# Attention with the batches in turn, and the last 256 tokens as dense slots, in an attention and mixture-of-experts block

## The chip, the cores and the metric

The kernel runs on one core of a Trainium2 chip. The metric is the device time of one execution in microseconds (us). Five engines work side by side, each with an instruction queue of its own: PE (matrix products), DVE (vector operations), ACT (activation functions), POOL (small operations and indirect DMAs) and SP (it issues most DMAs).

## The reference

The input x has 2 batches of 1024 tokens with 128 features. All values are float32. Cut to what matters:

```python
x = x + layernorm(attention(layernorm(x)))      # causal, 8 heads in 2 groups, latent keys and values of 32
x = x + layernorm(ffn(layernorm(x)))

def ffn(h):                                      # per token
    scores = sigmoid(h @ gate_weight.T)          # 32 experts in 4 groups of 8
    # the 2 best groups by the sum of their two best (scores + bias),
    # then the 6 best experts inside these 2 groups
    tw = scores[top6] / sum * 0.2
    routed = sum over the 6 of tw * (silu(h @ w_gate[e]) * (h @ w_up[e])) @ w_down[e]
    shared = silu(h @ shared_w_gate) * (h @ shared_w_up) @ shared_w_down
    anchor = the anchor expert that belongs to the best expert (one of 16)
    return routed + shared + 0.1 * anchor
```

So each token needs two of the four groups of experts, and which two depends on the data.

## The kernel before, in words

A token tile is 128 tokens; there are 8 in each batch, 16 in all. The kernel has four stages.

**Attention.** The work is cut into units (batch b, head group g, 256 queries q), and a unit into q+1 steps of 256 keys. `units` and `steps` fix the order: batch 0 with q = 0 to 3, then batch 1; 40 steps in all. A step has its scores (`numerators`, lines 541 and 555), the exponentials on ACT (561), in the last step of a unit a causal select on POOL (564), and in the following step the products with the values (578) and the sums (587). The maxima that a unit needs are computed ahead by PE (476, 486) and DVE (493). `project(b, c)` makes queries, keys and values of 512 tokens.

**Routing.** `route(i)` is run for each entry of `parts`: output projection (`po`, 712), two norms, transposes (`pt_h`, 746), gate products (`pl`, 752), and the choice of groups and experts on DVE. There are four parts of 4 tiles. Part 0 is not sorted (`ND = 1`), the others are: each token is copied twice into the DRAM tensor `placed`, once for each of its groups, so that each slot of 256 rows (`SL`) belongs to one group. The sorted tiles come in two sets, 8 tiles (`NT0`) and 4 tiles. `place_first` and `place_second` compute the places of a set on POOL (lines 895 to 947), and `move_rows` scatters its rows with indirect DMAs (955), one for each tile and choice.

**Dense pass.** `experts(0, 0)` takes the 512 tokens of part 0 through all four groups (lines 1317, 1318, 1331), with weights `wbd` and spread coefficients `spreadd`.

**Slots.** `Slots` runs 15 slots (`NS`), of which the first 5 (`NS0`) need the first set only. For each slot it fetches rows (`got`, 1095), transposes them (1105, 1107), writes the coefficients to DRAM (`cw_slot`, 1112), reads them back spread over partitions (`spreads`, 1126 and 1131), fetches the group's weights (`wbs`, 1047), multiplies (1148, 1156, 1157, 1171) and scatters the results (1180) to the DRAM tensor `results`. Both scatters and the reads of `placed` and `results` wait for each other as whole tensors; only scatters among themselves are declared free of dependencies. `finish(i)` adds the shared expert of a part (`psh`, 1213; `py`, 1249), reads the two results of each token back (`y`, 1268), and `normed` makes the last norm and stores.

**The order.** All engines take the program's order. What is not written out in sequence consists of generators, which stand in the queues `ends`, `moves` and `side`. A call of `tick()` takes one piece of `ends`, one of `moves` and `at_once` pieces of `side`; what a generator yields is the number of ticks until it may be taken again (0: not ready, and no turn is used). Attention calls `tick` about four times in a step, `Slots.run` three times for each pair of chunks of a slot. The batches' `qT` and `kT` buffers are later used for the weights (`wb_tags`). `tables` loads ACT's function table when a norm needs exponential and logarithm after a Silu.

The end of the program before sets the stages:

```python
    attention()
    at_once[0] = 2
    some = Slots()
    side += [place_first(), some.begin(), route(len(parts) - 1), place_second()]
    experts(0, 0)
    side += [finish(i) for i in range(ND, len(parts))]
    some.run()
```

Of the kernel before, what the change touches and what calls it, by code (L numbers as in the profile page):

```python
# [25 lines left out]
def attn_moe_block(  # L26
# [39 lines left out]

    nc = tc.nc
# [26 lines left out]
    parts = [(b, t, TB) for b in range(B) for t in range(0, NT, TB)]  # L94
    ND = 1
    sets = [parts[1:3], parts[3:]]
    NT0 = sum(n for _, _, n in sets[0])
    NTS = NT0 + sum(n for _, _, n in sets[1])
    NS = TOPG * NTS * P // SL + NG - 1
    NS0 = -(-(TOPG * NT0 * P - NG * (SL - 1)) // SL)  # L100
    NB0 = TOPG * NT0 * P // SL + NG - 1
    ROW = D + E + A + NG
# [14 lines left out]
    x_sb = [const.tile([P, NT, D], F32, name=f"x{b}") for b in range(B)]  # L117
    xr = [x[b].rearrange("(t p) d -> p t d", p=P) for b in range(B)]
    wq_sb = work.tile([P, NH, P], F32, tag="wide", name="wq_sb", bufs=3)
# [7 lines left out]
    half = NT // 2  # L127
    nc.sync.dma_start(out=x_sb[0][:, 0:half, :], in_=xr[0][:, 0:half, :])
# [7 lines left out]
    nc.sync.dma_start(out=x_sb[0][:, half:NT, :], in_=xr[0][:, half:NT, :])  # L136
    nc.sync.dma_start(out=wvd_sb, in_=wv_down)
    nc.sync.dma_start(out=wvup_sb, in_=wv_up)
# [3 lines left out]
    nc.sync.dma_start(out=x_sb[1], in_=xr[1])  # L142
# [31 lines left out]
    cw_rows = dram.tile([E + A, BC], F32, name="cw_rows")  # L174
# [89 lines left out]
    side, ends, moves = [], [], []  # L264
# [4 lines left out]
    def tick():  # L269
        nonlocal now  # L270
        now += 1
        for queue, most in ((ends, 1), (moves, 1), (side, at_once[0])):
# [130 lines left out]
    def project(b, c):  # L403
# [5 lines left out]
        norm.stats([x_sb[b][:, t, :] for t in tiles])  # L409
        if b:  # L410
            yield HOP
            yield from norm.roots()
        else:
            yield
            norm.root_act()
            yield
            norm.newton()
        for i, t in enumerate(tiles):
            (norm.apply_act if b else norm.apply)(xn[:, i, :], x_sb[b][:, t, :], i)
        yield b * HOP or 1  # L420
        xnT = work.tile([P, BC], F32, tag="xnT", name=f"xnT{b}{c}")
        transposed(xn, xnT, f"xn{b}{c}")
        yield b * HOP or 1
# [22 lines left out]
    units = [  # L446
        (b, g, q) for b in range(B) for q in range(NQ)
        for g in range(G)
    ]
# [162 lines left out]
    def attention():  # L612
# [39 lines left out]
        for k, (u, s) in enumerate(steps):  # L652
# [5 lines left out]
            if u[0] == B - 1 and u[2] * QC >= BC:  # L658
# [19 lines left out]
            tick()  # L678
            if any(need[j] - done > j - k - 1 for j in range(k + 1, len(steps))):
# [9 lines left out]
    hTs = {}  # L689
    rows = {}  # L690
    for b in range(B):
        hTs[b] = const.tile([P, T], F32, name=f"hT{b}")

    def route(i):


        b, t0, n = parts[i]
        sorts = i >= ND
        at = (i - ND) * TB
# [729 lines left out]
```

## Time and profile before

| | us |
|---|---|
| median of 3 runs | 460.83 (460.53 to 460.93) |
| the profiled execution's own time | 449.65 |
| its span | 448.0 |
| PE busy | 402.7 (90%) |
| DVE busy | 293.2 (65%) |
| ACT busy | 220.5 (49%) |
| POOL busy | 117.5 (26%) |
| attention ends, dense pass begins | 241.6 |
| slots begin | 301.7 |
| last matmul ends | 430.8 |

The durations below come from the profiled execution, whose clock of PE was 0.981 of full speed in the mean. A busy PE in this profile is not a PE at its peak, since ends of matmuls are modelled; the idle time is what can be read directly. In lists of waits the first name is who waits, the second whom it waits for, and the numbers are the sum, the count and the longest.

### The profile page before, as it was taken

The page shows a single profiled execution, that of the slowest core. Times are in us where ns is not written, and L with a number is a line of the kernel's source. Part 1 is how long each engine was busy: PE and PEld are TensorE (multiplying, and loading weights), DVE is VectorE, ACT ScalarE, POOL GpSimd, SP SyncE. Part 2 cuts the span into 40 slices and gives each one's busy share as a digit, 9 for nine tenths or more (in the row PEclk, how much of TensorE's full clock was granted, in tenths as well). Part 3 has the DMA queues.
Part 4 walks back from the last instruction along what each step waited for, and adds up shares of the span by engine and source line. Part 5 has one row for each costly group of instructions (what it writes and reads, how often), then busy time and mean ns, then how long its engine had stood idle before and what let it go on. Part 6 is the DMA issues. An engine that isn't in the chain of part 4 may idle for free.

```text
span 448.0 us, 10253 instructions
## 1 busy us (share of the span) xinstructions
PE 402.7 (90%) x3727; PEld 253.8 (57%) x3727; DVE 293.2 (65%) x1001; ACT 220.5 (49%) x469; POOL 117.5 (26%) x296
## 2 busy tenths in 40 slices
PE   8997899999999999998998999998789999997820
PEld 4554445645555555644554544447678899986620
DVE  5469852687699789799872576597433555455734
ACT  3454376276343577565566556436323433333621
POOL 4000100020001212022001688525852334241130
PEclk9999999999999999999999999999989999999995
DMA  7888000000000620000000257677278667787221
GB/s 216 186 235 174 2 0 2 1 4 1 1 2 1 173 75 2 1 1 2 1 2 2 53 179 215 174 218 217 93 219 242 207 209 239 220 246 232 83 63 55
DMA packets 46419, 47.63 MB, mean 106 GB/s; under 512 B 21152, under 2 KB 39312, under 8 KB 46368
## 3 DMA queue, kind: packets, MB, share of 16 engines
q1 hardware_dynamic: 42960, 41.51, 33.0%
q0 software_dynamic: 2112, 4.18, 2.8%
q10 hardware_dynamic: 1296, 1.28, 0.9%
q8 instruction: 30, 0.49, 0.5%
q14 instruction: 21, 0.17, 0.1%
HBM read 38.12 MB, written 11.45 MB: 111 GB/s over the span
## 4 chain that ended last, share of the span: by engine, by line
PE 51%; DVE 22%; DMA 12%; issue 6%; ACT 5%; POOL 2%; SPq 1%; ACTq 0%; POOLq 0%; DVEq 0%
DVE nm L493 9%; PE sm L476 7%; PE s L541 5%; DMA got<-placed 5%; PE o L578 4%; PE pgs L1148 4%; PE o L587 3%; PE pus L1148 3%; PE ys L1171 3%; PE pp L429 3%; PE pg L1317 3%; DMA y<-results 2%; PE oacc L1331 2%; PE pu L1318 2%; PE po L712 2%
## 5 line engine op out<-in xcount | busy, mean ns | idle before, releaser
L493 DVE TENSOR_REDUCE nm<-sm 128x1 f32<-128x512 f32 (+2 forms) x192 | 92.7, 548 | 35.2 <-PE sm L486 24.1
L561 ACT ACTIVATE pr<-s 128x512 f32<-128x512 f32 (+1 forms) x160 | 75.6, 558 | 71.8 <-PE s L555 71.8
L564 POOL TENSOR_SCALAR_AFFINE_SELECT pr<-pr 128x1024 f32<-128x1024 f32 x16 | 18.1, 1130 | 185.9 <-ACT pr L561 185.9
L541 PE MATMUL s<-qT,kT 32*128 32x256 f32 (+1 forms) x640 | 51.1, 383 | 4.6 <-DVE nm L493 3.8
L1156 DVE TENSOR_TENSOR hids<-hids,pus 128x512 f32<-128x512 f32 x30 | 20.6, 687 | 46.4 <-PE pus L1148 44.1
L1171 PE MATMUL ys<-wd_sb,hids 128*128 x300 | 41.0, 276 | 7.1 <-DVE hids L1157 5.3
L1180 POOL DMA_INDIRECT results<-ys,to_row x30 | 31.5, 1049 | 59.6 <-ACT ys L1177 37.0
L476 PE MATMUL sm<-kT,qT 32*128 32x512 f32 (+3 forms) x384 | 46.4, 525 | 0.6 <-DVE nm L493 0.4
L1171 PEld LDWEIGHTS ys<-wd_sb,hids 128*128 128x128 f32 x300 | 40.0, 191 | 10.9 <-DVE hids L1157 6.3
L541 PEld LDWEIGHTS s<-qT,kT 32*128 32x128 f32 x640 | 33.6, 184 | 21.4 <-issue 9.8
L578 PE MATMUL o<-pr,v 128*32 128x256 f32 (+1 forms) x640 | 39.4, 364 | 1.0 <-POOL preceded L855 1.0
L587 PE MATMUL o<-pr,ones 128*32 128x256 f32 (+1 forms) x640 | 39.3, 363 | 0.0
L1148 PE MATMUL pgs<-hTp,wbs 128*128 128x256 f32 x120 | 32.0, 390 | 1.2 <-issue 1.2
L1148 PE MATMUL pus<-hTp,wbs 128*128 128x256 f32 x120 | 30.9, 380 | 0.0
L578 PEld LDWEIGHTS o<-pr,v 128*32 128x32 f32 x640 | 16.7, 109 | 22.4 <-issue 10.3
L587 PEld LDWEIGHTS o<-pr,ones 128*32 128x32 f32 x640 | 17.2, 109 | 20.0 <-issue 10.6
L1157 DVE TENSOR_TENSOR hids<-hids,spreads 128x512 f32<-128x512 f32 (+1 forms) x45 | 27.2, 604 | 1.6
L955 POOL DMA_INDIRECT placed<-rows,place_of x24 | 24.5, 1020 | 7.5 <-issue 4.5
L1155 ACT ACTIVATE hids<-pgs 128x512 f32<-128x512 f32 x30 | 17.9, 598 | 15.3 <-PE pgs L1148 15.3
L476 PEld LDWEIGHTS sm<-kT,qT 32*128 32x128 f32 x384 | 18.2, 183 | 12.4 <-issue 3.6
L1148 PEld LDWEIGHTS pus<-hTp,wbs 128*128 128x128 f32 x120 | 23.1, 192 | 3.2
L1148 PEld LDWEIGHTS pgs<-hTp,wbs 128*128 128x128 f32 x120 | 21.2, 195 | 5.0 <-issue 2.9
(303 smaller groups left out, 628.1 us busy)
## 6 DMA issues: line engine op xcount, KB each, us to landing
wbs<-wgu SPq DMA_DIRECT2D x15, 640.0 KB, 4.4
spreads<-cw_slot SPq DMA_DIRECT2D x30, 256.0 KB, 4.0
spreadd<-cw_rows SPq DMA_DIRECT2D x16, 256.0 KB
got<-placed SPq DMA_DIRECT2D x15, 180.0 KB, 3.7
placed<-zero SPq DMA_DIRECT2D x1, 2640.0 KB
wbd<-wgu SPq DMA_DIRECT2D x4, 640.0 KB, 7.2
spreads<-cw_slot SPq DMA_DIRECT2D x60, 32.0 KB, 3.5
y<-results SPq DMA_DIRECT2D x3, 512.0 KB, 3.7
```

The source lines that it names most:

```text
L476: nc.tensor.matmul(banks[r][:, at : at + k1 - k0], lhsT=qT[ts(r, L), g, ts(qt, P)], rhs=kT[ts(r, L), g, k0:k1], start=(at == 0), stop=Fals ...
L493: nc.vector.tensor_reduce(nm[:, k0 // BC, j, r : r + 1], banks[r][:, at : at + k1 - k0], AX.X, ALU.max, negate=True,)
L541: nc.tensor.matmul(banks[r][:, at : at + n], lhsT=kT[rows, g, ts(kt, P)], rhs=qT[rows, g, q * QC + lo : q * QC + lo + n], start=(i == 0), ...
L561: nc.scalar.activation(pr[:, r, 0:m], banks[r][:, 0:m], AF.Exp)
L578: nc.tensor.matmul(o[ts(r, L), lo : lo + n], lhsT=qkv[b][2][:, kt, ts(g, L)], rhs=pr[:, r, at : at + n], start=(kt == 0), stop=False, skip ...
L587: nc.tensor.matmul(o[ts(r, L), QC + lo : QC + lo + n], lhsT=ones32, rhs=pr[:, r, at : at + n], start=False, stop=True, skip_group_check=True,)
L955: move = nc.gpsimd.indirect_dma_start(out=placed[:, :], out_offset=bass.IndirectOffsetOnAxis(ap=place_of[:, k, t : t + 1], axis=0), in_=ro ...
L1148: nc.tensor.matmul(p[:, lo : lo + SL], lhsT=wb[:, m, ts(c, P)], rhs=hT, start=(lo == 0), stop=(c == pair[-1]), skip_group_check=True,)
L1156: nc.vector.tensor_tensor(hid[:, 0:n], hid[:, 0:n], up, ALU.mult)
L1157: nc.vector.tensor_tensor(hid[:, 0:n], hid[:, 0:n], sp[:, pair[0] : pair[-1] + 1, :].rearrange("p c t -> p (c t)"), ALU.mult,)
L1171: nc.tensor.matmul(o[:, ts(j, D)], lhsT=hid[:, at : at + P], rhs=w, start=(c == 0 and j == 0), stop=(c == NC - 1), skip_group_check=True,)
L1180: move = nc.gpsimd.indirect_dma_start(out=results[:, :], out_offset=bass.IndirectOffsetOnAxis(ap=self.to_row[i][:, j : j + 1], axis=0), in ...
```

## The change

The units are ordered by `QT`: both batches with q = 0 and 1, then q = 2 of both, then q = 3 of both. The 16 tiles of x stand in one buffer in that order, and `parts` become (0,4), (4,4), (8,4), (12,2) and (14,2): position and number of tiles in that order. All but the last are sorted: 8 tiles in the first set, 6 in the second, so that `NS` is 17 and `NS0` is 5 still. The last part, 256 tokens, is taken through all groups as four more slots (indices 17 to 20), which read their tokens from `hTs` and their coefficients from `cw_rows`, and which add into one accumulator; `finish` adds that accumulator from PSUM. `experts` is gone. `place_first`, its scatters and `begin` (which fetches for the first two slots) now stand in queues during attention: `moves`, and a new queue `begins`. The POOL work of `place_first` is cut into pieces by yields. In `Slots`, the fixed points of fetching give way to `fetch`, which issues what is due and ready. Cut to its core:

```diff
+    QT = [(b, q) for b in range(B) for q in (0, 1)] + [(b, q) for q in (2, 3) for b in range(B)]
+    order = [(b, q * TQ + j) for b, q in QT for j in range(TQ)]
+    parts = [(0, 4), (4, 4), (8, 4), (12, 2), (14, 2)]
+    LAST = len(parts) - 1
+    sets = [range(0, 2), range(2, LAST)]
...
-        for queue, most in ((ends, 1), (moves, 1), (side, at_once[0])):
+        for queue, most in ((ends, 1), (moves, 1), (begins, 1), (side, at_once[0])):
...
-    units = [
-        (b, g, q) for b in range(B) for q in range(NQ)
-        for g in range(G)
-    ]
+    units = [(b, g, q) for b, q in QT for g in range(G)]
...
-            if u[0] == B - 1 and u[2] * QC >= BC:
+            if k > 5:
                 at_once[0] = 2
...
             tick()
+            if k > len(steps) - 8:
+                tick()
+                tick()
...
     def move_rows(t0, t1, done):
-        yield
...
-                yield
+                yield 1 if attending[0] else 2
+        yield HOP
         routed.add((done, "moved"))
...
     def place_first():
-        while any(("weights", ND + i) not in routed for i in range(len(sets[0]))):
+        while any(("weights", i) not in routed for i in sets[0]):
             yield 0
...
-        more_than(full, far, NT0 * P // SL)
-        more_than(new, total, NT0 * P // SL)
+        yield from more_than(full, far, NT0 * P // SL)
+        yield from more_than(new, total, NT0 * P // SL)
...
-        moved(0, NT0, rank, "a")
+        yield from moved(0, NT0, rank, "a")
         moves.append(move_rows(0, NT0, "first"))
         routed.add(("first", "placed"))
-        yield HOP + 1
+        side.insert(0, number_first())
...
         def begin(self):
+            while self.at["spread"] < 2:
+                self.fetch(-1, 2, 6)
+                yield
+                self.unit += 1
...
+        def fetch(self, i, k, gap):
+            at, when = self.at, self.when
+            def there(what, i):
+                return ("second" if i >= NS0 else "first", what) in routed
+            def old(what, i):
+                return self.unit >= when.get((what, i), -gap) + gap
+            limits = (
+                ("rows", i + 2 + (k > 0), NS, lambda j: there("moved", j) and there("numbered", j)),
+                ("weights", i + 2, NS + NG, lambda j: j >= NS or there("numbered", j)),
+                ("turn", i + 2, NS + NG, lambda j: j >= NS or ("rows", j) in when and old("rows", j)),
+                ("spread", i + 1 + (k > 1), NS + NG,
+                 lambda j: j >= NS and ("weights", LAST) in routed or ("turn", j) in when and old("turn", j)),
+            )
+            for what, upto, end, ready in limits:
+                while at[what] <= min(upto, end - 1) and ready(at[what]):
+                    getattr(self, what)(at[what])
+                    when[what, at[what]] = self.unit
+                    at[what] += 1
...
         def run(self):
             ahead = []
-            for i in range(NS):
+            for i in range(NS + NG):
+                while self.at["spread"] <= i:
+                    tick()
+                    self.unit += 1
+                    self.fetch(i, 0, 2)
                 for k in range(-(-NC // 2)):
                     ahead.append((i, k, self.hidden(i, k)))
                     if len(ahead) > 2:
                         self.down(*ahead.pop(0))
...
+                    self.unit += 1
+                    self.fetch(i, k, 2)
                     for _ in range(3):
                         tick()
...
+        if i == LAST:
+            while some.done < NS + NG:
+                yield 0
             tables(EXP_LN)
+            nc.vector.tensor_tensor(
+                own.rearrange("p t d -> p (t d)"), own.rearrange("p t d -> p (t d)"),
+                some.acc_of[NS][:, 0 : n * D], ALU.add,
+            )
         else:
+            while some.done < (NB0 + i if i in sets[0] else NS):
+                yield 0
...
+    some = Slots()
+    side += [first, project(1, 0), fold_values(), project(0, 1), project(1, 1)]
+    side += [route(i) for i in range(LAST)]
+    begins.append(some.begin())
+    moves += [place_first(), place_second()]
     attention()
+    attending[0] = False
     at_once[0] = 2
-    some = Slots()
-    side += [place_first(), some.begin(), route(len(parts) - 1), place_second()]
-    experts(0, 0)
-    side += [finish(i) for i in range(ND, len(parts))]
+    side += [route(LAST)] + [finish(i) for i in range(len(parts))]
     some.run()
```

## The prediction

> **What bounds the kernel now.** I read the whole span, then its stages, then the edges between the stages. Page lines (TensorE, then its busy tenths in 40 slices), then busy time by stage:
>
> ```profile
> span 448.0 us, 10253 instructions
> PE 402.7 (90%) x3727; PEld 253.8 (57%) x3727; DVE 293.2 (65%) x1001; ACT 220.5 (49%) x469; POOL 117.5 (26%) x296
> PE   8997899999999999998998999998789999997820
> ```
>
> ```profile
> core 0: us, PE busy (x) PEld busy (x) DVE busy (x) ACT busy (x) POOL busy (x), PEclk, DMA share, GB/s
> 17.60:101.30 83.70, 78.99 (x914) 42.60 (x912) 56.16 (x176) 45.25 (x104) 8.44 (x12) 1.00 0.28 67
> 101.30:241.60 140.30, 135.34 (x1880) 73.98 (x1876) 112.99 (x464) 79.39 (x179) 16.72 (x33) 1.00 0.08 21
> 241.60:301.70 60.10, 58.59 (x174) 27.37 (x171) 41.15 (x144) 32.39 (x53) 34.01 (x91) 1.00 0.53 155
> 301.70:350.30 48.60, 41.97 (x241) 35.88 (x240) 23.80 (x56) 20.91 (x43) 25.35 (x63) 0.96 0.65 191
> 350.30:405.00 54.70, 54.55 (x343) 49.97 (x342) 27.77 (x47) 19.92 (x46) 19.23 (x38) 1.00 0.75 226
> 405.00:430.80 25.80, 18.67 (x112) 15.74 (x110) 17.67 (x52) 12.38 (x24) 6.47 (x12) 1.00 0.44 138
> 430.80:448.00 17.20, 0.00 (x0) 0.00 (x0) 4.56 (x18) 3.03 (x6) 2.02 (x3) 0.61 0.17 53
> ```
>
> The reader should see a TensorE kernel with three leaks. Attention (to 241.6) and the dense pass over 512 tokens (60.1 us) keep PE busy. Slots 0 to 4 (301.7 to 350.3) leave PE idle for 6.6 us, the stretch from 405.0 for 7.1 us, and the last 17.2 us have no matmul. The undisturbed slot is read from the chain, where the first matmuls of slots follow each other by 6.98 us:
>
> ```profile
> 358.59 0.87 PE pgs L1148 x4
> 365.57 0.87 PE pgs L1148 x4
> 372.56 0.86 PE pgs L1148 x4
> ```
>
> The waits, and the timelines of PE and POOL, name two of the leaks. First, rows of sorted tokens are read back while the second set is still being scattered: a read waits for every scatter issued before it, and a scatter for a read. Second, DVE sits in `finish` waiting for `y`, and the next scatter waits for that read:
>
> ```profile
> SPq L1095 <- DMA placed<-rows,place_of: 16.0, 3, 9.4
> ```
>
> ```profile
> 326.04 0.69 PE L1105 MATMUL pt_s<-ident,got 128*128 128x128 f32 x2 [2.96 <-DMA got<-placed]
> ```
>
> ```profile
> 326.75 0.96 POOL L955 DMA_INDIRECT placed<-rows,place_of  x1 [2.09 <-DMA got<-placed]
> ```
>
> ```profile
> DVE y L1277 <- DMA y<-results: 14.1, 2, 8.8
> POOL results L1180 <- DMA y<-results: 14.5, 2, 7.6
> ```
>
> [...] 1283 ns per load; the trace has 1283 for all, so a norm between Silus costs ACT two loads, 2.6 us.
>
> **The change, part by part.** All sums are against the profiled execution: span 448.0, its own time 449.65. The median of the runs is 460.83, 2.5% more; I take that as proportional (as a fixed 11.2 us it would move my figure by 0.4).
>
> *The dense pass goes:* −60.1. It also covered the ranking and scattering of the first set (POOL busy 34.0 us there); that cover is now attention.
>
> *Slots.* A slot is 6.99 us (20 `pgs`/`pus`/`pa` matmuls, 4.32; 20 `ys`, 2.23; four transposes, 0.44). NS goes from 15 to 17, and the last 256 tokens are four slots without transposes, 6.55 each. So 17 × 6.99 + 4 × 6.55 = 145.0 us instead of 60.1 + 15 × 6.99 = 165: twenty less, since 256 tokens instead of 512 visit all groups.
>
> *Attention, PE work.* Tiles routed in it go from 12 to 14: a tile is 0.50 (`po`) + 0.15 (`pt_h`) + 0.25 (`pl`) = 0.9, so +1.8. The transposes of `cw` of the dense part leave (−0.55), a ranking comes in (+0.3), also `turn` of slots 0 and 1 (+0.9) and PE's load of five group numbers (0.77 in the row of L982). Sum +3.2.
>
> *Attention, waits.* By counting the yields, four ticks to a step and six in the last seven, `place_first` starts in step 25 of 40, its 16 scatters are issued in steps 30 to 33, `rows` of slots 0 to 2 in step 34, their transposes at the end of step 35, the spreads in step 36. On POOL that is 16.3 us of small operations (249.1 to 265.4) and 16 × 1.27 = 20.3 us of scatters. A causal select of 1.1 us passes through that queue at the end of each unit, and `values` waits for it. The work is emitted one piece (1 to 2 us) a tick, and a select comes every 3 to 4 steps of 4.7 us, so it mostly fits. POOL should end about 19.5 us ahead of attention's end, rows land some 8 us later, and PE reaches their transposes about 14.5 us ahead of the end, 3 us before the rows: I take 2 us of wait (0 to 5), as PE's extra work delays it too. Spreads land at about the end, so slot 0 follows directly.
>
> *Attention, order.* Small units of both batches come first. DVE needs 5.4 us for a unit of q=0 (reductions, split, quotient) against 4.2 of PE, and 7.6 against 8.7 for q=1. The `project` of batch 1 is awaited in step 2 with nothing emitted between its pieces. But the start is shorter, as only one projection stands ahead of step 0. Before had 7.2 us of idle PE in its first 60. No row shows the new order; I take +2 (−3 to +8). Attention so ends at 241.6 + 3.2 + 4 = 248.8.
>
> *Slots 0 to 4.* `weights` of part 3 comes in step 39, so the second set's rank is on PE after slot 0's first pair, as before (303.8). Before, counted from slot 0's start: rank at 4.5, POOL's sums done at 12.4, scatters to 28.5, last landing 32.1, slot 5 at 48.6. Now six tiles: sums 0.5 more, 12 scatters instead of 8. Rows of slot 4 still wait for the scatters issued ahead of them (four instead of five), land at about 24, and hold PE as at 326.04. The other eight scatters (10.2 us) and two scatters of results (2.6) end at about 37, landing at 41, nine later than before. Slot 5's rows land at 44.5. PE gets to its transposes at 43.3 (from 24.8: rest of slot 2 4.8, slot 3 6.5, part of slot 4 4.0, two shared experts and routing 3.2), waits 1.2, and its spread (ACT copies, `cw_slot` 2.8 to 3.5, SP's six issues, landing 3.5) is there at 54, 2 late. Slot 5 starts in effect at 51: +2.4.
>
> *Slots 5 to 16:* 12 × 6.99 = 83.9. Shared experts of the other parts: `psh` 0.86 and `py` 1.1 for four tiles, half for two: 4.0.
>
> *Results.* Parts 0 and 1 are fetched behind slots 10 and 11 while scatters go on, as now: 5 us of DVE holding PE. Parts 2 and 3 are fetched after slot 16, in the dense slots, where no scatter follows: one DVE wait, 2.5. The last downs wait 1.5 for DVE as at 429.17. Sum 9.0 (5 to 13).
>
> *Dense slots:* 26.2. Their weights and spreads need no sorting. `route` of the last part falls in slots 0 to 4, where PE waits anyway.
>
> *Tail.* Before: scatter, landing, read back, then 9.3 us from the first add at 438.70. Now the last part adds its accumulator from PSUM and needs neither scatter nor read: 9.3 less half of the add, statistics, apply and residual (1.6) and less one add (0.7) = 7.0, against 17.2.
>
> **Sum:** 248.8 + 51 + 83.9 + 4.0 + 9.0 + 26.2 + 7.0 = 429.9. Of the two unlisted things, ACT's table loads for five output norms and SP's queue, I give one us: **431**, 17 less than 448. Time 432.6 in the profile, × 460.83 / 449.65 = **443.5**.
>
> **The rivals.**
> *All leaks closed.* If ordering costs nothing, rows are on time, and results hold nobody, attention ends at 244.8, slots 0 to 4 take 40, and results cost 5: 4 + 11 + 4 = 19 less, span 412, time 424. For: POOL has slack in attention (25.2 of 224 us busy). Against: the chain of 12 scatters, landing, rows, spread takes 54 us and nothing in the sum hides it. A half of it gives 434.
> *The pipeline is only moved.* The sort of the first set comes late, slot 0 waits for rows, `cw_slot` and spread (about 10 us), and the second set's eight scatters behind the read of slot 4 hold slot 5 by another 5: 431 + 10 + 5 = 446 in span, time 459. For: every link there is a wait in today's trace. Against: the count of ticks leaves rows eleven us of margin.
> *Slower: POOL's sort is exposed in attention.* 36.6 us of POOL work goes into its steps 26 to 34 in the queue that the causal select shares. If selects stand behind it, `values` waits, and all of PE. It decides from 17 us of exposed waiting, about half of that work; wholly exposed gives span 467.6 and time 481. [...] 36.6 us in some 45 us of steps is 80% of POOL. Against: pieces are a tick apart, and `values` follows half a step behind its select.
> *It does not do what it says.* Should `spread(0)` not be issued in attention, `run` waits for it; that is the second rival's case.
>
> **How the numbers follow.** The forecast (span 422 to 440, time 434 to 453) has 0.60, closed leaks 0.13, only moved 0.15, slower 0.12. A measurement can tell about 0.2% (0.9 us) from no change. Low end 429, half-way into the closed leaks; high end 459, the end of the moved pipeline. Within the moved case 0.02 lies inside 0.2%. So faster 0.86, same 0.02, slower 0.12.
>
> **What would show it.** Attention's last `o` matmuls at 246 to 252 and `pgs` directly behind. The first `pgs` of slot 5 some 50 us later, with waits of `pt_s` on `got`. Slots then at 7.0 us and four at 6.55. POOL's scatters in attention with selects at most some us late. The last matmul seven us ahead of the end. Wrong if `o` waits long for POOL, if slot 0 waits for its spread, or if small units open gaps above 8 us in the first 60.

## The result, and the profile after

The changed kernel takes **481.69 us** in the median of 4 runs (480.46 to 482.47), beside 460.68 (460.34 to 460.93) before: a ratio of 1.0454, 95% interval 1.0429 to 1.0479. It is slower by 4.5%; 443.5 was forecast, with a range of 429 to 459. The profiled execution took 482.47 us, its span is 480.8. Its page begins so (span, busy time, TensorE's busy tenths in 40 slices, and the tenths of full speed that its clock was granted):

```profile
span 480.8 us, 10675 instructions
PE 422.4 (88%) x3856; PEld 284.3 (59%) x3856; DVE 295.4 (61%) x1033; ACT 225.9 (47%) x489; POOL 124.3 (26%) x328
PE   8886999999998999999596897689899997899754
PEclk9978699999997999999689599699999998999878
```

PE has more busy time than before although, by the prediction's sum, slots and dense part give it 20 us less to do. Part of it is the clock: sixteen `o<-pr,v` passes take 0.86 us at 225.26, where the clock is 1.00, and 1.94 us at 243.33, where it is 0.50. The dips of `PEclk` at the start, in the middle and at the end are new. By stage (attention up to 283.7, slots 0 to 4, slots 5 to 16, dense slots, tail; the start of attention cut at 60):

```profile
core 0: us, PE busy (x) PEld busy (x) DVE busy (x) ACT busy (x) POOL busy (x), PEclk, DMA share, GB/s
17.60:60.00 42.40, 35.34 (x304) 18.70 (x303) 24.15 (x91) 14.89 (x37) 2.21 (x2) 0.76 0.72 138
60.00:101.30 41.30, 40.59 (x475) 22.82 (x471) 25.49 (x73) 25.36 (x58) 4.53 (x4) 1.00 0.01 2
101.30:283.70 182.40, 163.79 (x2052) 85.88 (x2051) 133.33 (x560) 91.86 (x213) 49.47 (x140) 0.92 0.11 32
283.70:338.70 55.00, 46.44 (x262) 39.90 (x259) 29.94 (x105) 32.05 (x59) 30.78 (x75) 0.91 0.46 132
338.70:434.30 95.60, 89.38 (x538) 80.08 (x537) 52.31 (x111) 39.22 (x86) 28.03 (x54) 0.98 0.79 230
434.30:474.00 39.70, 31.95 (x174) 28.17 (x173) 21.87 (x58) 15.25 (x25) 3.85 (x7) 0.87 0.41 113
474.00:480.80 6.80, 0.00 (x0) 0.00 (x0) 2.61 (x12) 0.99 (x3) 0.00 (x0) 0.74 0.07 19
```

From 17.6 us to its end, attention leaves PE idle for 26 us where it left 10 before, and its clock is no longer 1.00 throughout. The undisturbed slot is as before, 6.99 us from one slot's first matmuls to the next's (the chain that ended last):

```profile
378.93 0.86 PE pgs L1209 x4
...
385.92 0.87 PE pgs L1209 x4
```

The waits that held PE before (the read of rows behind scatters, and `y`) are still there, the first in SP's list and the second in the general one. `ys` behind the products of DVE has grown, and `pt_h` behind ACT's `rows` is new (SP's list of the changed kernel, its general list, and the `ys` line of before):

```profile
SPq L1154 <- DMA placed<-rows,place_of: 19.8, 2, 13.2
```

```profile
PE ys L1236 <- DVE hids L1218: 12.7, 5, 4.9
DVE y L1353 <- DMA y<-results: 12.1, 4, 5.8
POOL results L1248 <- DMA y<-results: 8.2, 1, 8.2
PE pt_h L772 <- ACT rows L406: 5.6, 1, 5.6
```

```profile
PE ys L1171 <- DVE hids L1157: 5.3, 3, 2.7
```

The largest loss has no named wait. It is a stretch of 13 us in attention (timeline):

```profile
226.79 0.96 POOL L989 DMA_INDIRECT placed<-rows,place_of  x1 [0.19 <-issue]
228.05 0.96 POOL L989 DMA_INDIRECT placed<-rows,place_of  x1 [0.19 <-issue]
229.33 1.12 PE L497 MATMUL sm<-kT,qT 32*128 32x512 f32 x2 [1.85 <-issue]
...
234.38 0.62 PE L608 MATMUL o<-pr,ones 128*32 128x128 f32 x2 [0.86 <-issue]
...
237.11 0.96 POOL L989 DMA_INDIRECT placed<-rows,place_of  x1 [0.19 <-issue]
...
240.16 2.48 DVE L514 TENSOR_REDUCE nm<-sm 128x1 f32<-128x512 f32 x4 [12.38 <-remote]
240.44 0.59 ACT L615 COPY raw<-o 128x512 f32<-128x512 f32 x1 [8.32 <-remote]
```

POOL issues one scatter each 1.27 us, undisturbed. PE, after nine passes at the start of the stretch, does one to three matmuls at a time, some 0.7 or 1.4 us apart, and waits for nothing that the profile knows ("issue"). VectorE starts nothing for 12.4 us, ScalarE nothing for 8.3 ("remote": the profile names no releaser). I call this the **crawl**, and its sign is idle time of PE without a named wait. The windows around it show what it costs:

```profile
221.50:226.50 5.00, 5.00 (x66) 2.95 (x66) 4.12 (x8) 0.50 (x2) 4.45 (x9) 1.00 0.84 263
226.50:240.00 13.50, 6.89 (x27) 2.25 (x23) 1.24 (x17) 2.28 (x4) 9.88 (x22) 0.69 0.26 90
240.00:245.00 5.00, 4.94 (x33) 2.42 (x32) 4.64 (x21) 3.40 (x7) 0.00 (x0) 0.50 0.37 111
```

There are 27 passes of PE in 13.5 us; at the rate of the window ahead of it there would be about 180. Half clock follows (0.50 from 240 to 245).

### The profile page after: what moved, and what is told of

The parts are those of the page before. It is cut to its first block, busy times and chain, and to the rows that moved or that the text cites. A ratio compares the mean times of both kernels' runs of the same rounds, so it can differ in the third digit from the quotient of the medians.

```text
span 480.8 us, 10675 instructions
## 1 busy us (share of the span) xinstructions
PE 422.4 (88%) x3856; PEld 284.3 (59%) x3856; DVE 295.4 (61%) x1033; ACT 225.9 (47%) x489; POOL 124.3 (26%) x328
## 4 chain that ended last, share of the span: by engine, by line
PE 52%; DVE 16%; issue 12%; ACT 8%; DMA 7%; POOL 3%; SPq 1%; ACTq 0%; DVEq 0%; POOLq 0%
DVE nm L514 8%; PE ys L1236 8%; PE sm L497 7%; PE pgs L1209 5%; PE pus L1209 5%; PE s L562 5%; PE o L599 4%; PE pp L453 3%; PE o L608 3%; PE pa L1209 2%; DMA spreads<-cw_rows 2%; POOL placed L989 2%; DMA y<-results 2%; PE po L738 1%; DMA spreads<-cw_slot 1%
## 5 line engine op out<-in xcount | busy, mean ns | idle before, releaser
L1236 PE MATMUL ys<-wd_sb,hids 128*128 (+1 forms) x420 | 60.3, 286 | 17.7 <-DVE hids L1218 12.7
L1236 PEld LDWEIGHTS ys<-wd_sb,hids 128*128 128x128 f32 x420 | 58.5, 200 | 24.0 <-DVE hids L1218 12.9
L1217 DVE TENSOR_TENSOR hids<-hids,pus 128x512 f32<-128x512 f32 x42 | 28.8, 686 | 55.5 <-PE pus L1209 35.8
L1248 POOL DMA_INDIRECT results<-ys,to_row x34 | 35.7, 1051 | 76.6 <-ACT ys L1245 54.0
L497 PE MATMUL sm<-kT,qT 32*128 32x512 f32 (+3 forms) x384 | 50.3, 560 | 3.2 <-issue 1.9
L608 PE MATMUL o<-pr,ones 128*32 128x256 f32 (+1 forms) x640 | 44.2, 381 | 3.6 <-issue 3.6
L1218 DVE TENSOR_TENSOR hids<-hids,spreads 128x512 f32<-128x512 f32 (+1 forms) x63 | 38.0, 604 | 7.1 <-DMA spreads<-cw_slot 5.0
L1216 ACT ACTIVATE hids<-pgs 128x512 f32<-128x512 f32 x42 | 25.0, 597 | 37.0 <-PE pgs L1209 26.5
L1209 PE MATMUL pgs<-hTp,wbs 128*128 128x256 f32 x136 | 37.3, 399 | 1.5 <-issue 1.5
L1209 PE MATMUL pus<-hTp,wbs 128*128 128x256 f32 x136 | 36.0, 388 | 0.0
```

Source lines behind the costliest of these rows:

```text
L497: nc.tensor.matmul(banks[r][:, at : at + k1 - k0], lhsT=qT[ts(r, L), g, ts(qt, P)], rhs=kT[ts(r, L), g, k0:k1], start=(at == 0), stop=Fals ...
L608: nc.tensor.matmul(o[ts(r, L), QC + lo : QC + lo + n], lhsT=ones32, rhs=pr[:, r, at : at + n], start=False, stop=True, skip_group_check=True,)
L1209: nc.tensor.matmul(p[:, lo : lo + SL], lhsT=wb[:, m, ts(c, P)], rhs=hT, start=(lo == 0), stop=(c == pair[-1]), skip_group_check=True,)
L1217: nc.vector.tensor_tensor(hid[:, 0:n], hid[:, 0:n], up, ALU.mult)
L1218: nc.vector.tensor_tensor(hid[:, 0:n], hid[:, 0:n], sp[:, pair[0] : pair[-1] + 1, :].rearrange("p c t -> p (c t)"), ALU.mult,)
L1236: nc.tensor.matmul(o[:, ts(j, D)], lhsT=hid[:, at : at + P], rhs=w, start=(c == 0 and j == 0 and i <= NS), stop=(c == NC - 1 and (i < NS o ...
```

## The experiments

For attention I give the time from the first to the last `o<-pr,ones` matmul: 211.1 before, **250.4** after. The first of them comes at 30 to 38 us, a difference that this leaves out. "Step k takes" means the time from the first such matmul of step k − 1 to that of step k. Steps 1 and 2 together still take 25.8 to 30.0 us in executions whose start is the same, so attention is known to some 4 us only. The scatters fall into the steps 30 to 35, and there the three executions without scatters agree within 0.1 us (27.9 in e2, f1 and h3); this stretch is the finer measure.

Total times of single runs stand against 481.69. The runs were made on several chips, where the kernel before took 452.2 to 461.4 us, so totals are rough to some 2%, and the stretches decide.

### The order, and the place of the sort

The order alone, in the kernel before:

```diff
+    QT = [(b, q) for b in range(B) for q in (0, 1)] + [(b, q) for q in (2, 3) for b in range(B)]
-    units = [(b, g, q) for b in range(B) for q in range(NQ) for g in range(G)]
+    units = [(b, g, q) for b, q in QT for g in range(G)]
```

> The kernel before with the new order of units alone: routing, sorting, dense pass and slots as before. Attention ended at 241.6 us before and at 283.7 after the change. Theory 1 (short gaps of PE, each paid again by a stretch at half clock; the new order opens some of them between 24 and 56 us): attention ends 8 to 14 us later than 241.6. Theory 2 (what is sorted during attention is what costs; the order is free): attention within 3 us of 241.6.

483.23 us. Attention takes 216.3, so the order costs 5.2 in this one execution. The rest of the loss is elsewhere: slots begin 27.5 us behind the last dense matmuls `pg` (5 before), since the parts of the kernel before are then finished late and the sort has lost its cover. The total is thus no measure of the order in the changed kernel; the 5.2 is the better one.

The sort behind attention:

```diff
-    begins.append(some.begin())
-    moves += [place_first(), place_second()]
     attention()
+    begins.append(some.begin())
+    moves += [place_first(), place_second()]
```

> The changed kernel with the sort of the first set and the fetches of the first two slots taken up only after attention. Theory 2: attention ends at 250 us or earlier instead of 283.7, since the sort is the cost. Theory 1: only the slow stretch from 226 to 240 goes with its half clock, attention ends at 265 to 270. Both: with nothing to cover it, the sort (rank 8, sums 16, scatters 20, rows and spreads 15 us) stands open ahead of slot 0, so the whole is 20 to 45 us longer than the changed kernel.

510.94 us. Attention takes 231.9, 18.5 less. So sorting in attention costs 18.5 us there, and the rest of the change 15.6 more than the order alone. The sort uncovered costs more: slot 0 begins at 331.5.

### Which part of the sort

The weights fetched only after the scatters:

```diff
-                ("weights", i + 2, NS + NG, lambda j: j >= NS or there("numbered", j)),
+                ("weights", i + 2, NS + NG, lambda j: j >= NS or there("moved", j) and there("numbered", j)),
```

> The changed kernel with the weights of the first two slots fetched only when the first set's scatters have landed, ten ticks later. Between 226 and 240 us all engines but POOL stood nearly still in the changed kernel, with no wait in the profile, beginning when these 1.3 MB and the scatters had run together. If the two together cause it: the stretch goes, attention ends 14 to 17 us earlier than 283.7 and the whole is 12 to 17 us shorter. If scatters alone cause it, or the load of the group numbers: attention within 3 us of 283.7.

482.44 us, attention 247.7, VectorE's stall again 12.4 us, though the fetches are now issued at 240.9 us, behind the last scatter, instead of 221.6. The 640 KB fetches are not the cause.

The scatters alone, or the group numbers alone, held back:

```diff
     def move_rows(t0, t1, done):                 # f1
+        while attending[0]:
+            yield 0
     def number_first():                          # f2
+        while attending[0]:
+            yield 0
```

> The changed kernel, with the ranking of the first eight tiles and the load of the group numbers left in attention and only their 16 scatters held back until attention is over. Theory: the stretch of 226 to 240 us, in which TensorE, VectorE and ScalarE crawl while POOL issues scatters, is made by the scatters. Then it is gone, its half clock with it, and the last o matmul comes near 268 us instead of 283 (12 to 16 us earlier). Rival: it is made by the load of the group numbers into registers, which ends just ahead of it; then it is still there and attention ends at 281 to 284. In both cases slot 0 comes later (its rows are scattered only then), and the whole takes longer than 482 us, 490 to 505.

> The changed kernel, with the 16 scatters left in attention and the load of the first group numbers into registers (and the fetches of weights and rows that need it) held back until attention is over. Theory of the scatters: the crawl of 226 to 240 us stays and attention ends at 280 to 284 us. Rival, the register load makes it: the crawl is gone and attention ends near 268. In both cases slot 0 waits for numbers, weights, rows and spreads after attention, some 10 us more, the whole at 485 to 497 us.

f1: 500.14 us, attention **230.1**, the crawl gone. f2: 496.49 us, attention **249.7**, VectorE's stall 12.3 us. Both ran on the same chip, and in both the fetching of rows and what follows from it is held back too, so the difference is the scatters. Ranking, numbers and register loads cost attention next to nothing: f1 has them, e2 has not, and the steps 10 to 35 take 133.8 and 133.4 us.

Two ticks of distance, or a pause on POOL's own queue:

```diff
-                yield 1 if attending[0] else 2       # g1
+                yield 2
+                if attending[0]:                     # h1
+                    nc.gpsimd.memset(pause, 0.0)     # 128x512, twice
+                    nc.gpsimd.memset(pause, 0.0)
```

> The changed kernel, with each of the first 16 scatters two ticks behind the last instead of one: about 2.3 us apart instead of 1.35, so from 216 to some 253 us. Theory: the crawl of TensorE, VectorE and ScalarE sets in because scatters follow each other without a pause (it begins about with the ninth and ends with the last); spaced out, VectorE's stall of 12.4 us is gone or under 4 us, and attention ends at 266 to 274 us instead of 283. Rival: any scatters in attention do it, whatever their distance; then the crawl is as long as their train, longer than now, and attention ends at 283 to 295. Whole time 468 to 476 by the first (slot 0 still finds its rows), 482 to 495 by the second.

> The changed kernel with two memsets of 128x512 on POOL behind each of the 16 scatters in attention, on its own queue, so that the distance is kept also where POOL has fallen behind (with two ticks of distance the trace showed trains of 12 scatters 1.27 us apart all the same, since POOL first waited for a causal select and then caught up). Theory: a train of scatters without a pause makes TensorE, VectorE and ScalarE crawl from about its fourth or eighth on. With some 2.3 to 2.5 us from one to the next the crawl is gone, VectorE has no stall above 4 us in that stretch, and attention ends at 266 to 272 us instead of 279 to 283. Rival: the crawl depends on scatters in flight, not on their pace; then it is there as before or longer, attention ends at 280 or later.

g1: 479.55 us, attention 241.7. It spaced little: behind the first two, POOL waited for a causal select and then issued ten scatters some 1.27 us apart; VectorE stalled for 10.6. The last four came 20 us later, without a crawl.

h1: 480.07 us, attention 247.0. By its numbers the pace makes no difference: attention ends at 283.9, and steps 33 and 34 take 15.0 and 12.5 us, where f1 has 5.6 and 3.5. Its trace says otherwise. The scatters are 2.3 us apart, and **the crawl is gone**: between steps 29 and 35 PE has no gap without a named wait (6.7 us of them in the changed kernel) and 16.0 us of waits with a name. The largest of them (timeline of h1):

```profile
239.06 0.12 POOL L807 MEMSET gs<- 128x16 f32 x1
239.21 0.37 DVE L820 MAX8 gtop<-gs 128x8 f32<-128x8 f32 x4 [9.04 <-POOL gs L807]
...
240.89 1.65 PE L739 MATMUL po<-ao,ot 128*128 128x128 f32 x6 [6.87 <-DVE ot L630]
...
256.49 0.66 PE L1169 MATMUL pt_s<-ident,got 128*128 128x128 f32 x2 [6.82 <-DMA got<-placed]
```

VectorE waits 9.0 us for a small memset of the routing, which stands on POOL's queue behind the scatters and their pauses; PE then waits for VectorE, and later for rows that land late. From 241 to 252 us, with five more scatters issued, PE does 90 passes. So the pace does matter: pauses end the crawl and put the cost into POOL's queue instead.

The same bytes as plain writes from SP, in the kernel f1:

```diff
+                nc.sync.dma_start(
+                    out=aside[ts(k * NT0 + t, P), :], in_=rows[i][:, t - parts[i][0], :]
+                )
+                yield 1
```

> The kernel with the scatters held back until attention is over, to which 16 plain writes of the same rows (128 x 720 bytes each, to a scratch tensor in the device's memory) are added on SP's queue at the places in attention where the scatters were. It tells transfers from their issue on POOL. If the writes themselves, their bytes or their signals, make the engines crawl, attention ends at 276 to 284 us. If it is the indirect issue on POOL, it ends at 264 to 269 as without them (266.8).

498.47 us, attention **231.0**, steps 30 to 35 at 27.9. The plain writes do no harm. They are a weaker test than they look, since SP ran ahead: four went out at 159 to 161 us, four at 187 to 188, and only eight close together, at 218.6 to 224.4. Sixteen of them in one train were not tried. The runs fit a difference between scatters from POOL and plain writes from SP (30.7 us for steps 30 to 35 with eight scatters, in i1 below, 27.9 with eight close plain writes), but they do not show what in the two makes it.

Only eight in attention, or the same sixteen in another order:

```diff
         for k in range(TOPG):                        # i1
+            while k and attending[0]:
+                yield 0
-        for k in range(TOPG):                        # i2
-            for t in range(t0, t1):
+        for t in range(t0, t1):
+            for k in range(TOPG):
```

> The changed kernel with the first eight of the 16 scatters in attention and the other eight held back until attention is over. In all traces with scatters in attention the crawl sets in with the ninth (at 226.8 us of the changed kernel, at 244 with the pauses) and ends with the sixteenth. Theory: the first eight are free and the later ones are what the engines pay for; then there is no stall of VectorE above 4 us between 210 and 250 us and attention ends at 264 to 270. Rival: the crawl comes with a given place in the program (the steps 31 to 34, or the scatters' overlap with the routing of the third part), whatever the count; then some of it is left and attention ends at 272 to 283.

> The changed kernel with the two scatters of a tile behind each other (first and second choice of tile 0, then of tile 1, ...), instead of all first choices and then all second ones. The ninth scatter was also the first one of a second choice. If it is the count that matters, the crawl again begins with the ninth and attention ends at 278 to 284 us. If it is the second choice (the same rows read again, rows of another block written), it begins with the second scatter, is spread over the train, and VectorE's long stall begins some 9 us earlier.

i1: 484.34 us, as slot 0 now waits for the other eight, but attention takes **229.6**, about as without scatters. i2, on the same chip: 478.35 us, attention 244.9, VectorE's stall 12.3 us, from the ninth on as before. (In the changed kernel the ninth is the one at 228.05; the 226.8 of the expectation is the eighth. What it dates to 244 with the pauses is h1's named waits.) With eight, the same stretch of the program looks so (windows of i1):

```profile
217.00:222.00 5.00, 4.22 (x50) 1.58 (x42) 3.78 (x22) 2.01 (x4) 3.10 (x9) 1.00 0.58 229
222.00:240.00 18.00, 16.82 (x251) 9.03 (x243) 16.92 (x80) 8.86 (x21) 2.79 (x10) 1.00 0.01 3
```

251 passes of PE in 18 us at full clock. Eight are not quite free, though: PE has a gap of 0.8 us without a named wait behind the start of the eighth scatter, and step 31 takes 6.3 us instead of f1's 4.2. In the changed kernel and in i2, f2 and e3, too, PE's first such gap begins just ahead of the record of the ninth (0.6 to 0.9 us), so the crawl sets in with the eighth, and what follows prolongs it.

| scatters in attention | runs | steps 30 to 35, us |
|---|---|---|
| none | e2, f1, h3 | 27.9 |
| eight, 1.27 us apart | i1 | 30.7 |
| sixteen, 1.27 us apart | changed kernel, f2, e3, i2 | 43.8, 43.5, 43.7, 44.9 |
| twelve, then four 20 us later | g1 | 40.1 |
| sixteen, 2.3 us apart, no crawl | h1 | 49.5 |

So **eight scatters cost 2.7 us there, and eight more in the same train 13 to 14**, in either order. In the trace of the changed kernel each scatter from the ninth on waits for the semaphore that the one eight before it raises (111 to 118 in turn), the first eight for none of these; POOL's idle time ahead of a scatter is 0.16 to 0.19 us from the second on, with that wait and without. The first execution of the kernel before has the same waits and no stall (VectorE idle for 2.1 us at most while the scatters go out), so they alone do not make it. What holds the other engines remains open.

The kernel before, once more:

> The kernel before, unchanged, for a second profiled execution of it, since the one that the prediction was summed against took 449.65 us and its median is 460.8. If the 11 us are one stall, of a kind that the changed kernel also has (a stretch of some 12 us in which TensorE, VectorE and ScalarE all crawl), it shows here as one stretch of half clock and idle engines in attention that the first profile has not. If they are spread, every stage is 2% longer. Span 448 or 458 to 459 us.

458.11 us, span 456.3. Its dense pass has something like the crawl too, shorter, during its own first sixteen scatters: VectorE is idle for 7.0 us, ScalarE for 4.2 and PE for 1.3, the last two without a named wait (windows, and timeline of VectorE in f0):

```profile
241.80:309.20 67.40, 61.04 (x182) 27.34 (x171) 42.02 (x147) 32.15 (x53) 33.21 (x92) 0.99 0.49 145
```

```profile
287.17 0.69 DVE L1322 TENSOR_TENSOR hid<-hid,pu 128x512 f32<-128x512 f32 x1 [7.04 <-PE pu L1318]
```

That stage took 60.1 us in the execution that the prediction was summed against, 67.4 here: most of the 8.3 us between the spans. In i3 below, whose scatters are those of the kernel before, it took 66.8. So the stage with the same train of sixteen is long in two executions and not in a third. The one chip on which the kernel before took 452.2 us may be like the third; its executions of that kernel have no trace here.

### The start, and the half clock

> The changed kernel, with dummy matmuls (44, about 9.5 us of TensorE at full clock) behind and ahead of the scores of steps 0 to 2 and in each tick that waits for the projection of batch 1. Theory: in the first 60 us it is not the waits themselves that cost, but the half clock that follows them (24.7 to 31.5, 38.4 to 41.8 and 45.2 to 55.4 us, 20.4 us at half speed, so 10 lost). The dummies hold the clock up, those windows shrink to under 7 us in sum, and step 3 is reached 3 to 7 us earlier (67 us instead of 70.8), attention ends at 276 to 281. Rival: the chain of VectorE and ScalarE sets the pace there; then the clock rises but step 3 comes no earlier, or later by up to 4 us.

```diff
                 tick()
+                awake(5)                             # in the wait for a projection
+            if k < 3:
+                awake(4)                             # ahead of numerators and behind
```

483.17 us. The clock is up (windows of f3):

```profile
17.60:60.00 42.40, 38.42 (x342) 19.99 (x334) 25.31 (x95) 14.85 (x35) 2.21 (x2) 1.00 0.61 133
```

1.00 instead of 0.76, but step 3 is reached at 72.5 us instead of 70.8. Counted from step 0's `o` it takes 34.7 instead of 37.7, and executions without dummies take 33.5 to 37.7, so a gain cannot be told from their differences, and 10 us are not in it. The **rival held** as to the result: the clock rose and step 3 came no earlier. That VectorE and ScalarE set the pace there is the likely reason; no run shows it. In this stretch of the changed kernel the mean clock was 0.76 although the longest wait of PE was only 2.0 us.

> The changed kernel, where in steps 0 to 7 a unit's maxima are taken ahead only if its projection is already emitted. In the changed kernel step 2 issues the maxima of unit (1,0,0) early, so four empty ticks and the whole projection of batch 1 stand on TensorE's queue ahead of step 2. Theory: it is this order on TensorE's queue, a chain of VectorE and ScalarE with nothing else emitted in between, that makes the first 84 us slow, not the half clock. Steps 2 to 5 then take 6 to 10 us less: step 9 is reached at 100 to 104 us instead of 109.7, and the whole time falls to 472 to 477 us. Rival: VectorE and ScalarE are the bound of the small units; then step 9 comes at 107 to 110 and the whole time is 479 to 483.

```diff
-            if done < len(items):
+            if ready_item(k):      # steps 0 to 7: only where the projection is emitted
```

The same guard stands at the second place that takes maxima ahead. 475.81 us, attention **238.7**. Step 2 comes 3.3 us behind step 1 instead of 20.1, but most of it is given back: steps 4 to 7 take 42.7 us instead of 28.8. Step 9 comes 69.4 us behind step 0, against 72.5 to 76.6 in executions with the old start, so 3 to 7 us are the edit's. That part of the loss is the order on PE's queue: the changed order of units makes the maxima of batch 1 due in step 2, and PE then stands behind a projection of which each piece waits for ScalarE (2.0 us at 46.2, 0.7 at 48.5 and 0.7 at 53.0 in the changed kernel).

### The ticks at the end of attention

```diff
-            if k > len(steps) - 8:
-                tick()
-                tick()
```

> The changed kernel without the two added ticks in each of the last seven steps. Theory 1: the wait of 5.6 us at pt_h (the routing of part 3 comes so fast that PE reaches its transposes ahead of the norm) goes, and with it the half clock of 263 to 274 us, so attention ends 8 to 11 us earlier than 283.7; part 3 is routed later, so slot 5 gains less, and the whole is 0 to 6 us shorter. Theory 2: attention within 2 us of 283.7, the whole longer by up to 9 us.

491.81 us. Attention falls to 241.8: step 36 takes 4.7 us instead of 13.1, since PE no longer waits for `rows` of the fourth part (5.6 us in the changed kernel). But the second sort comes later, slot 5 begins 71.6 us behind slot 0 instead of 55.0. The extra ticks cost some 8 us in attention (24.0 instead of 16.0 behind step 35) and save 16.6.

### Reading y later

```diff
-            yield 4
+            yield 8
             both = both.rearrange("p (t k d) -> p t k d", t=n, k=TOPG)
```

> The changed kernel, where the two results of each token are added eight ticks after they were fetched instead of four. Theory: VectorE's waits for y (5.85 us at 402, 3.90 at 448.2, 2.12 at 454.2) hold up what stands behind them, the two products of hids and ScalarE's next Silu, and so cost TensorE its waits of 3.20, 2.82 and 4.89 us and the half clock behind each. Then VectorE waits for y for under 3 us in all, the stretch from slot 5 to the end of the dense slots takes 6 to 11 us less, and the time is 471 to 476. Rival: what delays the dense slots is ScalarE's switching of tables for two output norms that overlap; then the waits for y go and the time falls by under 3 us, to 479 or more.

474.62 us. The waits halve (the general list of g3):

```profile
DVE y L1353 <- DMA y<-results: 6.3, 3, 4.3
PE ys L1236 <- DVE hids L1218: 4.6, 2, 4.4
```

From the first dense matmul to the last one it is 34.7 us instead of 39.6, so 4.9 are the edit's. The rest of the 7 came in attention and the start, which it does not touch. The kernel before with the same edit:

> The kernel before with one edit, y read eight ticks after its fetch instead of four. If what g3 showed holds there too (VectorE's wait for y holds up the products of the slots), the stretch from 400 to 430 us shrinks by the 5.3 us that VectorE waits for y there or a part of it, and the time falls by 2 to 5 us, 0.4 to 1.1%. If the wait is covered, it falls by under 1 us.

458.02 us in the median of 20 runs against 459.36 of 23: ratio 0.9968, 95% interval 0.9943 to 0.9994. It is faster by 0.3%, less than the 2 to 5 us hoped for. Of the versions tried it is the only one ahead of the kernel before.

### Together

g4 has g1, g2, g3 and the residual of attention on VectorE:

```diff
-            own_eng().tensor_tensor(part, part, an[:, t : t + 2, :], ALU.add)
+            nc.vector.tensor_tensor(part, part, an[:, t : t + 2, :], ALU.add)
```

h2 has g2, g3, this, h1's pause, and one extra tick instead of two.

> The three edits at once (scatters two ticks apart, no stall for the projection, y read eight ticks later) and the residual of the attention output added on VectorE instead of POOL, where two additions run beside the shared work of VectorE at 142 us and TensorE then waits 2.0 us. If the causes are separate, the gains add: 9 to 17 of the scatters, 6 to 10 of the projection, 6 to 11 of y, 2 of the residual, so 445 to 460 us, about as fast as the kernel before or faster. If they share their cover (a gain in one place is given back in waiting for rows, spreads or the second sort), the whole time stays above 465.

> The changed kernel with five edits: no stall for the projection, y read eight ticks later, the attention residual on VectorE, the pause between scatters, and one extra tick instead of two in the last seven steps of attention (with two, route of the fourth part comes in four steps and TensorE waits 5.6 us for its rows at 260 us; with none, its sort comes late). If the pause works and gains add: attention ends at 255 to 262 us and the slots take 188 to 196 from there, so a time of 446 to 458, against 460.7 before: faster than the kernel before by 1 to 3%. If the pause does not work: attention ends at 268 to 275 and the time is 460 to 470.

g4: 468.19 us, h2: 466.71 us in the median of 4 runs, a ratio of 1.0308 (1.0259 to 1.0356) to the kernel before on that chip (452.24). Beside the kernel before on the same chip, that is 1.015 for g4 (one run each side, 461.44) and 1.031 for h2, instead of 1.045. g4 still has the crawl. h2, with the pause, has none, but the same chain as h1: VectorE waits 8.4 us for POOL's memset, PE then 6.8 for VectorE, and later 4.9 for rows. Neither beats the kernel before.

## Why the prediction was wrong, point by point

The sum was 431 for the span (times 460.83 / 449.65 this gives a time of 443.4, not 443.5), 49.8 too little: attention 34.9, slots 0 to 4 4.0, slots 5 to 16 2.7, dense slots 9.4, less 1.2 for the tail and the unlisted us.

- **"Attention, waits": 2 us (0 to 5). This step failed.** It asked whether POOL's queue would be late for its neighbours, and priced the scatters on POOL alone, 16 × 1.27. In the changed kernel PE waited 1.0 us for POOL. What the step left out is that scatters in a close train can hold engines that wait for nothing of POOL's: steps 30 to 35 take 43.8 us with them and 27.9 without (f1), so they cost 15.9 there. The rest of the 20.3 us between the two attentions is 2.5 in steps 1 and 2, where executions differ anyway, and 1.9 at the end. The profile of before showed sixteen scatters beside busy engines, since that one execution happened to have no stall.
- **"Attention, PE work": +3.2.** Only PE's busy time was priced. The moved projection and routing also put waits on PE's queue: f1 against e1 leaves 13.8 us, with the uncertainty of the start. The parts that were tried one by one: 3 to 7 for the projection in step 2 (g2; it shares them with the order) and some 8 for routing in the extra ticks (e4). I did see the projection awaited in step 2 with nothing between its pieces, and gave it no price.
- **"Attention, order": +2 (−3 to +8).** 5.2 in e1, one execution, within its range.
- **"Slots", 6.99 and 6.55.** Right where nothing disturbs them: 6.99 for slots 9 to 12 and 6.55 for slots 15 to 18, by the first `pgs` of each; slots 5 to 8 take 7.5 to 9.5. **Slots 0 to 4:** 55.0 for 51. **Slots 5 to 16 with results:** 95.6 for 92.9.
- **Dense slots, 26.2 and 4.0 of waits.** 39.6: mis-sized by 9.4, of which g3 gave back 4.9. VectorE waits for `y` with the products of the next `hids` behind it, twice (3.9 us at 448.2, 2.1 at 454.2), and then ScalarE, which has to switch its tables for two output norms (four loads of 1.28 us between 445.2 and 460.8), comes late with a Silu (VectorE waits 3.6 us for it at 461.45).
- **Tail, 7.0.** Right: 6.8.
- **The slower rival** named 481 us and the time was 482. That the number fits is luck: it had causal selects stand behind the sort on POOL, and PE's waits for POOL in that part are 1.0 us in all. Waits behind POOL's queue became large only in h1 and h2, where pauses made that queue longer.
- The gain that was counted on did come: fewer rows and a short tail. It went to attention, which was thought free.

## What to carry to other kernels

Work that is moved under a full stage has to be priced on every engine that shares the stage, not only on the one that does it; where no row shows it beside such work, the whole of its duration is a safer guess than nothing. Before a queue is reordered, look for what each engine will stand behind: waiting early for one projection cost 3 to 7 us, beside the prediction's 3.2 for all the added arithmetic. A total alone does not tell whether an experiment worked: h1 ended as late as the changed kernel, for another reason, and only the names of the waits show it. The low clock at the start (0.76) went with waits of PE; filling them with dummy matmuls brought it to 1.00 and gained nothing that could be told.

## What the runs showed of the hardware

Eight indirect scatters of 128 rows of 720 bytes, 1.27 us apart, cost the other engines 2.7 us between steps 29 and 35 of attention (30.7 in i1, 27.9 with none); eight more in the same train cost another 13 to 14, with VectorE still for 12 us and idle time that has no named wait. At 2.3 us apart (h1, h2) no such idle time is seen, and waits for POOL's queue take its place. Such a train does not always stall the others: of three traces with the scatters of the kernel before, two have a long dense pass (67.4 us in f0, with VectorE idle for 7.0 at once, and 66.8 in i3) and one has not (60.1).

In the crawl POOL kept its 0.96 us a scatter while the others stood; no run shows what they stood for. One explanation stands untested. The profile has a landing for each of the sixteen scatters in the first execution of the kernel before, and for none of them in f0 and in the changed kernel, so records are missing where the stalls are (in i1, almost without a stall, most are missing too). Whether the recording itself takes part in the stall is not known. Why the others stand is open.
